# Graph attention over 16 batches: whole-array matmuls gathered into three blocks of a batch, and the layernorm split over two engines

## The chip, the core and the metric

The kernel runs on one core of a Trainium2 chip. Its engines are TensorE (matmuls and transposes, PE in the profile), VectorE (DVE), ScalarE (ACT), GpSimd (POOL) and SyncE (SP, which here only issues DMAs). The metric is device time of one execution in microseconds: 2637.62 us, the median of three runs (2637.59 to 2637.79). A difference of about 0.2% is what such runs can tell from no change.

## What is computed

Two residual layers over x of 16 batches x 1024 nodes x 256 channels, in float32, each followed by a layernorm over the channels. The change lies in the first layer and at the seam to the second:

```
fea = transpose(x)                                  # per batch: channels x nodes
c = mean(fea, axis=1)
diff = c[:, None, :] - c[:, :, None]
A = abs(abs(sigmoid(diff) - 0.5) - 0.5) * 2.0       # symmetric weights from means
g = relu(einsum('bcn,bnm->bcm', fea, adj * A_s) * para)
q = heads(transpose(g));  k, v = heads(x @ kv_w)    # 4 heads of 64
out = softmax(q k^T * scale) v
x = layernorm(x + out)
# layer 1
x = layernorm(x + batchnorm(relu(batchnorm((A_hat x) W1^T + b1)) W2^T + b2))
```

## The kernel before

**Units and bursts.** Attention of a batch is cut into 32 units: two pairs of heads (pr), two halves of the queries (qh), eight key chunks of 128 (m). `scores` (L895) makes a 128 x 1024 tile of scores with four matmuls that each use a 64 x 64 quarter of the array, and ScalarE takes the exponential (L908) into a tile p (four buffers). `outputs` (L911) multiplies p by the values, again on quarters (L924), and VectorE adds p into an accumulator acc for the denominators (L931, L933). In the profile every float32 matmul is recorded twice, and a group of quarters runs side by side. Two units make a burst, sixteen bursts (u = 0 to 15) a batch. In each burst the scores of burst j come first and then the outputs of burst j - 1 (`back`, L1135), so that the exponentials have the time of a group of outputs.

**Whole-array work.** Between bursts stands work that uses the whole 128 x 128 array, for the batch after the current one (its `steps`) and the one after that (its `first`):

- `transpose_x` (L758): four groups of four transposes, x to xT. Before the first, `begin` (L743) sums x over the channels on VectorE and sends the means through DRAM, to come back as a row on all partitions (crow).
- `values` (L848) and `keys` (L836): four groups each, v and kT, copied out of PSUM by VectorE and ScalarE.
- `graph_mm` (L797): the product of x with the weights wg, in four parts for each of the four (c, half) results; each result is 128 x 512 in one PSUM bank, and `queries` (L812) takes it out: VectorE multiplies by para (L814), ScalarE takes the relu (L817).
- `normalise` (L940): ones times acc, the sums over keys (den), which go through DRAM to lie as columns (dcol). `residual` (L964): four transposes of the output oT (poT), a multiplication by the reciprocal on VectorE (o, L974, one buffer), and an addition into x on GpSimd (L979).

The weights wg are the `side` work, on ScalarE (`weights_abs` L782, `weights_tanh` L787) and VectorE (`weights_adj` L791), eight tiles each.

`finish_x1` (L981) is the layernorm of a batch: eight statistics and aggregations on VectorE, two operations on GpSimd for the reciprocal root (L587, L589), eight subtract-and-multiply on VectorE (L600); then a DMA to DRAM, and only after this can the x of a later batch be loaded into the buffer.

**PSUM.** Three pools of two buffers each: s (two banks a buffer, scores and some others), t (one bank: transposes, v, k, graph results, den, poT) and o (one bank, the outputs).

**What sets the order.** The order of TensorE, ScalarE and VectorE is the order of the calls (`manual_schedule`); each engine's program is in that order, and an instruction waits on semaphores for what it needs. The loop over bursts gives the bursts u = 0, 4, 6, 8, 10 and 12 (`FULL`) each a block of four steps, with transposes of the next x at u = 10 and 12, the residuals four bursts after their last unit (at u = 4 and 12), and the layernorm at u = 5, between two bursts. The side work is in u = 13, 14, 15, 0, 1, 2, 3 and 4.

**The last two batches.** Batch 14 has no later x to transpose; it takes on sums of adj's rows and of its diagonal (`adjacency_rows` L1038, `adjacency_diagonal` L1031, both on VectorE). Batch 15 has no graph work; in its bursts 0, 4, 6 and 8 stand transposes of adj (`transpose_adjacency` L1041, tiles pah, copied out by ScalarE). After the last burst come the first product of layer 1 (`aggregate_first` L1092), the last residuals and the layernorm of batch 15, and then layer 1, whose bound is again TensorE.

Of the kernel before, what the change touches and what calls it, by code (L numbers as in the profile page):

```python
# [10 lines left out]
F32 = mybir.dt.float32  # L11
I32 = mybir.dt.int32
AF = mybir.ActivationFunctionType
ALU = mybir.AluOpType
# [4 lines left out]
P = 128  # L19
# [496 lines left out]
def fast_path(  # L516
# [46 lines left out]
    def tile_t(name):  # L563
        return psum["t"].tile([P, HALF], F32, tag="t", name=name)
# [26 lines left out]
    def layernorm(t, name):  # L591
# [7 lines left out]
        for n in range(NCH):  # L599
            nc.vector.tensor_scalar(  # L600
                t[:, n, :], t[:, n, :], mv[:, n, 0:1], rstd[:, n : n + 1], ALU.subtract, ALU.mult
            )

    def products(name, bank, out, mm, temps, bias):

        t = {}

        def add(dst, ps, src, b):
            if b is None:
                nc.vector.tensor_add(dst, ps, src)
            else:
                nc.vector.scalar_tensor_tensor(dst, ps, b, src, op0=ALU.add, op1=ALU.add)

        up, low = bias or (None, None)

        def p1():
            t["a"] = bank(f"a_{name}")  # L620
            mm(1, t["a"], True)
            t["p1"] = temps("p1", name)
            nc.scalar.copy(t["p1"], t["a"])

        def p6():
            t["b"] = bank(f"b_{name}")
            mm(6, t["b"], True)
            t["u2"] = temps("u2", name)
            add(t["u2"], t["b"], t["p1"], up)

        def p2():
            mm(2, t["a"], False)
            if up is None:
                nc.scalar.copy(out[0], t["a"])
            else:
                nc.scalar.activation(out[0], t["a"], AF.Identity, bias=up)

        def p7():
            mm(7, t["b"], False)
# [60 lines left out]
    with (  # L700
# [2 lines left out]
        tc.tile_pool(name="pp", bufs=4) as pp,  # L703
        tc.tile_pool(name="accp", bufs=2) as accp,
        tc.tile_pool(name="rdp", bufs=1) as rdp,
        tc.tile_pool(name="op", bufs=3) as op,
    ):
        adj_s = adjp.tile([P, NCH, N], F32, tag="adj", name="adj_s")
        para_s = pap.tile([P, CC, N], F32, tag="pa", name="para_s")
# [23 lines left out]
        def prologue(b):  # L733
# [6 lines left out]
            def step(f, *a):  # L740
                steps.append((f, a))
# [14 lines left out]
                nc.sync.dma_start(s["crow"], c_d[b][0].partition_broadcast(P))  # L756

            def transpose_x(c, half):  # L758
                if c == 0 and half == 0 and b:
                    begin()  # L760
                if c == 0 and half == 0:
                    s["xT"] = xTp.tile([P, CC, N], F32, tag="xT", name=f"xT_{b}")
                pt = tile_t(f"pxT_{b}_{c}_{half}")
                for j in range(4):
                    nc.tensor.transpose(
                        pt[:, j * P : (j + 1) * P], xt[:, 4 * half + j, c * P : (c + 1) * P], ident
                    )
                nc.vector.tensor_copy(s["xT"][:, c, half * HALF : (half + 1) * HALF], pt)

            def row_of_means():  # L770

# [22 lines left out]
                    w, w, 1.0, adj_s[:, n, :], op0=ALU.subtract, op1=ALU.mult  # L794
                )

            def graph_mm(c, half, part):  # L797
                if part == 0:
                    s["pg"] = tile_t(f"pg_{b}_{c}_{half}")
                    if c == 0 and half == 0:  # L800
                        s["qT"] = qkv.tile([P, CC, N], F32, tag="qT", name=f"qT_{b}")
                ps = s["pg"]
                hs = slice(half * HALF, (half + 1) * HALF)
                for n in (2 * part, 2 * part + 1):
# [43 lines left out]
            def values(pair):  # L848
                if pair == 0:
                    s["v"] = qkv.tile([P, NCH, C], F32, tag="v", name=f"v_{b}")  # L850
                pt = tile_t(f"pv_{b}_{pair}")
                for j in range(2):
                    n = 2 * pair + j
                    for c in range(CC):
                        nc.tensor.matmul(  # L855
                            pt[:, j * C : (j + 1) * C], s["xT"][:, c, n * P : (n + 1) * P],
                            kvw_s[:, c, C : 2 * C], start=(c == 0), stop=(c == CC - 1),
                        )
                nc.vector.tensor_copy(
                    s["v"][:, 2 * pair : 2 * pair + 2, :].rearrange("p n c -> p (n c)"), pt  # L860
                )

            for i in range(2 * CC):
                first.append((transpose_x, (i // 2, i % 2) if b else (i % 2, i // 2)))
            if b == 0:
                first += [(begin, ()), (row_of_means, ())]
            for i in range(4):
                step(values, i)
                step(keys, i // 2, i % 2)
            for c in range(CC):  # L870
                for half in range(2):
                    for part in range(4):
                        if b:
                            step(graph_mm, c, half, part)
# [89 lines left out]
        def residual(b, pr, qh):  # L964
# [13 lines left out]
            xs = s["x"][:, 4 * qh : 4 * qh + 4, pr * P : (pr + 1) * P]  # L978
            nc.gpsimd.tensor_tensor(xs, xs, o.rearrange("p n h d -> p n (h d)"), ALU.add)  # L979

        def finish_x1(b):  # L981
            xt = st.pop(b)["x"]
            layernorm(xt, f"l0_{b}")
            nc.gpsimd.dma_start(x1_d[b], xt)

        def run(fs, k):
            for f, a in fs[:k]:
                f(*a)
            del fs[:k]
# [118 lines left out]

        BURST = 2
        bursts = [range(i, i + BURST) for i in range(0, len(units), BURST)]
        PERB = PER // BURST
        FULL = (0, 4, 6, 8, 10, 12)
        SIDE = {13: 2, 14: 2, 15: 2, 1: 2, 2: 2, 3: 2}
        with tc.manual_schedule(engines={mybir.EngineType.PE, mybir.EngineType.Activation, mybir.EngineType.DVE}):


# [3 lines left out]
            for _ in range(8):  # L1122
                run(steps, 1)
                run(side, 2)
            run(next_first, 4)
            for n in range(NCH):
                run(side, 2)
                run(steps, 1)
# [1 line left out]
                    run(next_side, 3)  # L1130
            run(next_side, 99)
            run(next_steps, 8)
            full, sums, late = {}, {}, {}

            def back(j):  # L1135

                for i in bursts[j]:
                    outputs(i)
                b, pr, qh, m = units[bursts[j][-1]]
                if m == NCH - 1 and qh == 1:  # L1140
                    sums.setdefault(j + 1, []).append((normalise, (b, pr)))
                    for q in range(2):
                        full.setdefault(j + 5, []).append((residual, (b, pr, q)))
                    if pr == PAIRS - 1:
                        late.setdefault(j + 6, []).append((finish_x1, (b,)))

            last = {
                0: [(transpose_adjacency, (m, h)) for m in (0, 1) for h in (0, 1)],
# [8 lines left out]
                15: [(scale_adjacency, (0,))],  # L1157
            }
            before_last = {
                6: [(adjacency_rows, (n,)) for n in (0, 1, 2)] + [(load_weights, ())],  # L1160
                8: [(adjacency_rows, (n,)) for n in (3, 4, 5)],
                10: [(adjacency_rows, (n,)) for n in (6, 7)],
                12: [(adjacency_diagonal, ())],
            }
            for j in range(len(bursts)):
                b, u = j // PERB, j % PERB
# [7 lines left out]
                run(late.get(j, []), 9)  # L1174
# [21 lines left out]
                run(sums.get(j, []), 9)  # L1196
            j = len(bursts)
            back(j - 1)
            for m in range(NCH):
                if m + 1 < NCH:  # L1200
                    scale_adjacency(m + 1)
                aggregate_first(m)
                run(sums.get(j + m - 1, []), 9)
                run(full.get(j + m, []), 9)
            for i in range(NCH // 2):
                adjacency_sums(i)
            run(late.get(j + 5, []), 9)

    attention_psum.close()

# [421 lines left out]
```

## Time and profile before

| what | value |
|---|---|
| time, median of three | 2637.62 us |
| profiled span | 2635.9 us |
| TensorE matmul busy | 2572.7 us, 98% |
| VectorE busy | 1587.8 us, 60% |
| ScalarE busy | 1110.2 us, 42% |
| GpSimd busy | 338.9 us, 13% |
| first score of batch 3 to first score of batch 4 | 104.91 us |
| of this: busy TensorE, VectorE, ScalarE | 104.32, 66.51, 54.74 us |

The profile page gives the busy share of each engine, a chain of what ended last, and groups of equal instructions with their mean duration and the idle time ahead of them. The timeline lists the instructions of a stretch in order of time: start, length of the merged piece, engine, line, output <- inputs, shape, count, and in brackets the idle time ahead of it and who ended it. "issue" in a bracket means that the profile shows no wait. A busy TensorE isn't a TensorE without gaps, since the end of a matmul is overlapped with the start of the next: distances from start to start tell more than busy time.

### The profile page before, as it was taken

Reading aid. Unit: us, or ns where it says so; the run is one execution under the profiler, and the core shown is the slowest. Engines: PE = TensorE matmul, PEld = TensorE weight load, DVE = VectorE, ACT = ScalarE, POOL = GpSimd, SP = SyncE. Lnnn points to the kernel's source line nnn. Section 1 sums busy time; section 2 is a strip of 40 time slices with the busy share of each in tenths; the row PEclk is TensorE's granted clock in tenths of the full one; section 3 lists DMA queues with packets and bytes.
Section 4 is the critical chain, followed back from the end, with each engine's and each line's share of the span. In section 5 each row is a group of like instructions: output and inputs, shape, how many; then the busy total and the mean of one; then the engine's idle time right before and its main releaser. Section 6 shows DMA issues by size and latency. Waiting matters only on the chain. (4 is left out here: it accounts for less than half of the span.)

```text
span 2635.9 us, 32325 instructions
## 1 busy us (share of the span) xinstructions
PE 2572.7 (98%) x13158; PEld 1118.6 (42%) x13158; DVE 1587.8 (60%) x2159; ACT 1110.2 (42%) x1321; POOL 338.9 (13%) x407
## 2 busy tenths in 40 slices
PE   8999999999999999999999999999999999999986
PEld 4443444444434444444344443334444444444455
DVE  5465665756656657566566576766565565533367
ACT  5363563644635636546356364501100111133358
POOL 0001000100000001001000010232221122000036
PEclk9999999999999999999999999999999999999999
DMA  4001101011011010110110110112222222254458
GB/s 144 2 9 41 33 10 41 17 25 33 9 41 33 10 41 19 23 33 9 41 33 9 41 49 2 41 55 89 96 76 84 86 90 96 96 201 150 159 194 303
DMA packets 134557, 168.96 MB, mean 64 GB/s; under 512 B 86784, under 2 KB 120064, under 8 KB 124032
## 3 DMA queue, kind: packets, MB, share of 16 engines
q1 hardware_dynamic: 129568, 116.47, 14.1%
q0 software_dynamic: 4832, 50.34, 4.6%
q8 instruction: 105, 1.72, 0.3%
q14 instruction: 52, 0.43, 0.0%
HBM read 99.36 MB, written 67.44 MB: 63 GB/s over the span
## 5 line engine op out<-in xcount | busy, mean ns | idle before, releaser
L908 ACT ACTIVATE p<-ps 128x1024 f32<-128x1024 f32 x512 | 495.6, 1020 | 179.7 <-PE ps L903 132.6
L933 DVE TENSOR_TENSOR acc<-acc,p 128x1024 f32<-128x1024 f32 x384 | 483.2, 1258 | 60.9 <-ACT p L908 32.3
L903 PE MATMUL ps<-qT,kT 64*64 64x512 f32 x4096 | 490.5, 594 | 1.4 <-ACT p L908 1.4
L924 PE MATMUL po<-p,v 64*64 64x512 f32 x4096 | 485.3, 589 | 0.0
L805 PE MATMUL pg<-wg,x 128*128 128x512 f32 x960 | 425.2, 596 | 0.0
L979 POOL TENSOR_TENSOR x<-x,o 128x512 f32<-128x512 f32 x64 | 109.5, 1711 | 1434.8 <-DVE o L974 1434.8
L924 PEld LDWEIGHTS po<-p,v 64*64 64x64 f32 x4096 | 156.7, 133 | 282.8 <-issue 282.6
L805 PEld LDWEIGHTS pg<-wg,x 128*128 128x128 f32 x960 | 177.6, 190 | 226.9 <-issue 203.3
L903 PEld LDWEIGHTS ps<-qT,kT 64*64 64x64 f32 x4096 | 146.1, 132 | 280.2 <-issue 231.5
L817 ACT ACTIVATE qT<-qT 128x512 f32<-128x512 f32 x64 | 40.1, 630 | 481.9 <-DVE qT L814 481.9
L1457 PE MATMUL po<-hl,w12T 128*128 128x512 f32 x512 | 222.0, 596 | 3.6 <-ACT hl L1387 2.8
L814 DVE SCALAR_TENSOR_TENSOR qT<-pg,para_s 128x512 f32<-128x512 f32 x64 | 43.9, 689 | 270.7 <-PE pg L805 269.8
L793 DVE SCALAR_TENSOR_TENSOR wg<-wg,adj_s 128x1024 f32<-128x1024 f32 x128 | 153.1, 1217 | 16.0 <-ACT wg L789 16.0
L1457 PEld LDWEIGHTS po<-hl,w12T 128*128 128x128 f32 x512 | 97.7, 191 | 127.9 <-issue 120.4
L784 ACT ACTIVATE wg<-crow,ccol 128x1024 f32<-128x1024 f32 x128 | 146.6, 1146 | 12.2 <-DMA crow<-c 12.2
L789 ACT ACTIVATE wg<-wg 128x1024 f32<-128x1024 f32 x128 | 135.5, 1059 | 2.6
L1387 ACT ACTIVATE hl<-hl,bn_sh,bn_sg 128x1024 f32<-128x1024 f32 x64 | 74.4, 1229 | 137.4 <-DMA hl<-h 136.1
L855 PE MATMUL pv<-kvw_s,xT 128*128 128x256 f32 x512 | 124.0, 385 | 1.6 <-ACT kT L846 1.6
L1468 DVE TENSOR_SCALAR o<-po,col_b 128x1024 f32<-128x1024 f32 x31 | 39.8, 1283 | 138.1 <-PE po L1457 138.1
L842 PE MATMUL pk<-xT,kvw_s 128*128 128x512 f32 x256 | 120.3, 592 | 0.0
L855 PEld LDWEIGHTS pv<-kvw_s,xT 128*128 128x128 f32 x512 | 94.9, 190 | 51.9 <-issue 27.6
L1286 PE MATMUL b_agg<-aT,x1S 128*128 128x512 f32 x240 | 109.2, 598 | 0.0
(159 smaller groups left out, 2641.4 us busy)
## 6 DMA issues: line engine op xcount, KB each, us to landing
h<-hw POOLq DMA_DIRECT2D x16, 2048.0 KB, 6.6
hl<-h SPq DMA_DIRECT2D x15, 2048.0 KB
x<-x POOLq DMA_DIRECT2D x16, 1024.0 KB, 4.2
x1l<-x SPq DMA_DIRECT2D x16, 1024.0 KB
xf<-x SPq DMA_DIRECT2D x16, 1024.0 KB
out_dram<-o SPq DMA_DIRECT2D x16, 1024.0 KB
x<-in_x_dram SPq DMA_DIRECT2D x15, 1024.0 KB
crow<-c SPq DMA_DIRECT2D x15, 512.0 KB
```

The lines of the kernel that those rows point to most:

```text
L784: nc.scalar.activation(w, s["crow"], AF.Abs, bias=s["ccol"][:, n : n + 1])
L789: nc.scalar.activation(w, w, AF.Tanh, scale=0.5)
L793: nc.vector.scalar_tensor_tensor(w, w, 1.0, adj_s[:, n, :], op0=ALU.subtract, op1=ALU.mult)
L805: nc.tensor.matmul(ps, xt[:, n, c * P : (c + 1) * P], s["wg", n][:, hs], start=(n == 0), stop=(n == NCH - 1),)
L842: nc.tensor.matmul(ps, kvw_s[:, c, kc * P : (kc + 1) * P], s["xT"][:, c, hs], start=(c == 0), stop=(c == CC - 1),)
L855: nc.tensor.matmul(pt[:, j * C : (j + 1) * C], s["xT"][:, c, n * P : (n + 1) * P], kvw_s[:, c, C : 2 * C], start=(c == 0), stop=(c == CC - 1),
L903: nc.tensor.matmul(ps[kh * D : (kh + 1) * D, hd * HALF : (hd + 1) * HALF], kT[r, pr, ks], qT[r, pr, qh * HALF : (qh + 1) * HALF], start=Tr ...
L908: nc.scalar.activation(p, ps, AF.Exp)
L924: nc.tensor.matmul(g["po"][kh][hd * D : (hd + 1) * D, :], s["v"][r, m, h * D : (h + 1) * D], p[r, hd * HALF : (hd + 1) * HALF], start=(m = ...
L933: nc.vector.tensor_add(g["acc"], g["acc"], p)
L979: nc.gpsimd.tensor_tensor(xs, xs, o.rearrange("p n h d -> p n (h d)"), ALU.add)
L1457: nc.tensor.matmul(ps[:, hs], w2T[:, k, c * P : (c + 1) * P], h[k][:, hs], start=(k == 0), stop=(k == HC - 1),)
```

## The change

The whole-array work of a batch is gathered into three blocks, after the bursts u = 0, 4 and 8. It is for fewer changes between quarters and whole array. Its parts:

- **u = 0**: seven of the eight v and k groups, with the denominators of the batch before and its four residuals (both pairs of heads) between them, and the rest of the side work.
- **u = 4**: the graph product of c = 0, all of it, then the eighth group (the last k). The layernorm of the batch before stands around it: statistics ahead of the block, and the scaling after four of its steps.
- **u = 8**: two transposes of the next x, half the graph product of c = 1, two more transposes, the other half, then den of the first pair.
- **Side work** moves to u = 9 to 15 (two items each) and u = 0.
- **Graph results** are 128 x 1024 in a buffer of pool s in place of 128 x 512 in pool t; VectorE and ScalarE take each out in one operation of 1024 columns in place of two of 512.
- **Layernorm** is split (`layernorm_steps`): statistics on VectorE, four operations on GpSimd in place of two (also minus mean times scale), and the scaling by eight ACTIVATE on ScalarE in place of eight VectorE operations.
- **Copies**: half of the xT copies and half of the v copies go from VectorE to ScalarE, from batch 1 on.
- **oT** has four buffers in place of three, since the first pair's residuals wait for u = 0 of the next batch.
- **Batch 14 and 15**: row sums go to u = 8, 10, 11, 12, 13 and the diagonal to u = 15; the lists of batch 15 stay, with its first pair's residuals at u = 12. `full`, `sums` and `late` are lists in order of entry in place of tables by burst.

```diff
+    def layernorm_steps(t, name):
...
+        def statistics():
+            for n in range(NCH):
+                nc.vector.bn_stats(st[:, n, :], t[:, n, :])
+                nc.vector.bn_aggr(mv[:, n, :], st[:, n, :])
+            rsqrt(rstd, mv[:, :, 1], EPS)
+            nc.gpsimd.tensor_tensor(nmr, mv[:, :, 0], rstd, ALU.mult)
+            nc.gpsimd.tensor_scalar(nmr, nmr, -1.0, None, ALU.mult)
+
+        def apply():
+            for n in range(NCH):
+                nc.scalar.activation(
+                    t[:, n, :], t[:, n, :], AF.Identity,
+                    bias=nmr[:, n : n + 1], scale=rstd[:, n : n + 1],
+                )
...
-        tc.tile_pool(name="op", bufs=3) as op,
+        tc.tile_pool(name="op", bufs=4) as op,
...
-                nc.vector.tensor_copy(s["xT"][:, c, half * HALF : (half + 1) * HALF], pt)
+                copy = nc.scalar.copy if half and b else nc.vector.tensor_copy
+                copy(s["xT"][:, c, half * HALF : (half + 1) * HALF], pt)
...
-            def graph_mm(c, half, part):
-                if part == 0:
-                    s["pg"] = tile_t(f"pg_{b}_{c}_{half}")
...
+            def graph_mm(c, n):
+                if n == 0:
+                    s["pg"] = tile_s(f"pg_{b}_{c}")
...
+                for hs in (H0, H1):
                     nc.tensor.matmul(
-                        ps, xt[:, n, c * P : (c + 1) * P], s["wg", n][:, hs],
+                        s["pg"][:, hs], xt[:, n, c * P : (c + 1) * P], s["wg", n][:, hs],
                         start=(n == 0), stop=(n == NCH - 1),
                     )
-                if part == 3:
-                    queries(c, hs, ps)
+                if n == NCH - 1:
+                    queries(c, slice(0, N), s["pg"])
...
+                copy = nc.scalar.copy if pair % 2 and b else nc.vector.tensor_copy
...
-        FULL = (0, 4, 6, 8, 10, 12)
-        SIDE = {13: 2, 14: 2, 15: 2, 1: 2, 2: 2, 3: 2}
...
             before_last = {
-                6: [(adjacency_rows, (n,)) for n in (0, 1, 2)] + [(load_weights, ())],
-                8: [(adjacency_rows, (n,)) for n in (3, 4, 5)],
-                10: [(adjacency_rows, (n,)) for n in (6, 7)],
-                12: [(adjacency_diagonal, ())],
+                6: [(load_weights, ())],
+                8: [(adjacency_rows, (n,)) for n in (0, 1, 2, 3)],
+                10: [(adjacency_rows, (4,))],
+                11: [(adjacency_rows, (5,))],
+                12: [(adjacency_rows, (6,))],
+                13: [(adjacency_rows, (7,))],
+                15: [(adjacency_diagonal, ())],
             }
...
-                if u in FULL:
-                    if u >= 10:
-                        run(next_first, 1)
-                    for _ in range(4 if b or u > 4 else 0):
-                        run(steps, 1)
-                        if u <= 4:
-                            run(side, 2)
-                    if u >= 10:
-                        run(next_first, 1)
-                    run(full.get(j, []), 9)
-                elif u > 12:
-                    run(next_side, SIDE[u])
-                else:
-                    run(side, SIDE.get(u, 0))
+                if u == 0:
+                    for i in range(7):
+                        if b:
+                            run(steps, 1)
+                            run(side, 1 if i < 4 else 2)
+                        if i == 1:
+                            run(sums, 1)
+                        if i in (2, 3, 5):
+                            run(full, 1)
+                    run(side, 99)
+                    run(full, 1)
+                elif u == 4:
+                    run(late, 1)
+                    keys_last = steps[:1] if b else []
+                    del steps[: len(keys_last)]
+                    for n in range(NCH):
+                        run(steps, 1)
+                        if n == 3:
+                            run(late, 1)
+                    run(keys_last, 1)
+                elif u == 8:
+                    run(next_first, 3)
+                    for n in range(NCH):
+                        run(steps, 1)
+                        if n == 3:
+                            run(next_first, 2)
+                    run(sums, 1)
+                elif u > 8:
+                    run(next_side, 2)
...
+                    if u == 12:
+                        run(full, 2)
```

More of the change, by code (lines that the diff above doesn't have):

```diff
@@ L602, in layernorm @@
             )
+    def layernorm_steps(t, name):
+        st = small.tile([P, NCH, 6], F32, tag="ln_st", name=f"st_{name}")
+        mv = small.tile([P, NCH, 2], F32, tag="ln_mv", name=f"mv_{name}")
+        rstd = small.tile([P, NCH], F32, tag="ln_rs", name=f"rs_{name}")
+        nmr = small.tile([P, NCH], F32, tag="ccol", name=f"nm_{name}")
+        def statistics():
[11 more added lines that the diff above has]
+                )
+        return statistics, apply
     def products(name, bank, out, mm, temps, bias):
@@ L758, in transpose_x @@
             def transpose_x(c, half):
-                if c == 0 and half == 0 and b:
-                    begin()
                 if c == 0 and half == 0:
@@ L795, in weights_adj @@
                 )
-            def graph_mm(c, half, part):
-                if part == 0:
-                    s["pg"] = tile_t(f"pg_{b}_{c}_{half}")
-                    if c == 0 and half == 0:
+            def graph_mm(c, n):
+                if n == 0:
+                    s["pg"] = tile_s(f"pg_{b}_{c}")
+                    if c == 0:
                         s["qT"] = qkv.tile([P, CC, N], F32, tag="qT", name=f"qT_{b}")
-                ps = s["pg"]
-                hs = slice(half * HALF, (half + 1) * HALF)
-                for n in (2 * part, 2 * part + 1):
+                for hs in (H0, H1):
                     nc.tensor.matmul(
-                        ps, xt[:, n, c * P : (c + 1) * P], s["wg", n][:, hs],
+                        s["pg"][:, hs], xt[:, n, c * P : (c + 1) * P], s["wg", n][:, hs],
                         start=(n == 0), stop=(n == NCH - 1),
                     )
-                if part == 3:
-                    queries(c, hs, ps)
+                if n == NCH - 1:
+                    queries(c, slice(0, N), s["pg"])
             def queries(c, hs, ps):
@@ L858, in values @@
                         )
-                nc.vector.tensor_copy(
-                    s["v"][:, 2 * pair : 2 * pair + 2, :].rearrange("p n c -> p (n c)"), pt
-                )
+                copy = nc.scalar.copy if pair % 2 and b else nc.vector.tensor_copy
+                copy(s["v"][:, 2 * pair : 2 * pair + 2, :].rearrange("p n c -> p (n c)"), pt)
             for i in range(2 * CC):
@@ L866, in prologue @@
                 first += [(begin, ()), (row_of_means, ())]
+            else:
+                first.insert(0, (begin, ()))
             for i in range(4):
@@ L869, in prologue @@
                 step(keys, i // 2, i % 2)
[L870 to L874, printed above, removed]
+            for c in range(CC if b else 0):
+                for n in range(NCH):
+                    step(graph_mm, c, n)
             for n in range(NCH if b == 0 else 0):
@@ L979, in residual, with statistics_x1 @@
             nc.gpsimd.tensor_tensor(xs, xs, o.rearrange("p n h d -> p n (h d)"), ALU.add)
+        def statistics_x1(b):
+            statistics, st[b]["ln"] = layernorm_steps(st[b]["x"], f"l0_{b}")
+            statistics()
         def finish_x1(b):
-            xt = st.pop(b)["x"]
-            layernorm(xt, f"l0_{b}")
-            nc.gpsimd.dma_start(x1_d[b], xt)
+            s = st.pop(b)
+            s["ln"]()
+            nc.gpsimd.dma_start(x1_d[b], s["x"])
         def run(fs, k):
@@ L1124, in fast_path @@
                 run(side, 2)
-            run(next_first, 4)
+            run(next_first, 5)
             for n in range(NCH):
@@ L1132, in fast_path @@
             run(next_steps, 8)
-            full, sums, late = {}, {}, {}
+            full, sums, late = [], [], []
             def back(j):
@@ L1140, in back @@
                 if m == NCH - 1 and qh == 1:
-                    sums.setdefault(j + 1, []).append((normalise, (b, pr)))
+                    sums.append((normalise, (b, pr)))
                     for q in range(2):
-                        full.setdefault(j + 5, []).append((residual, (b, pr, q)))
+                        full.append((residual, (b, pr, q)))
                     if pr == PAIRS - 1:
-                        late.setdefault(j + 6, []).append((finish_x1, (b,)))
+                        late.append((statistics_x1, (b,)))
+                        late.append((finish_x1, (b,)))
             last = {
@@ L1173, in fast_path @@
                     back(j - 1)
-                run(late.get(j, []), 9)
                 if u == 5 and b + 2 < B:
@@ L1177, in fast_path @@
                     next_first, next_steps, next_side = prologue(b + 2)
-                if u in FULL:
-                    if u >= 10:
-                        run(next_first, 1)
-                    for _ in range(4 if b or u > 4 else 0):
-                        run(steps, 1)
-                        if u <= 4:
-                            run(side, 2)
-                    if u >= 10:
-                        run(next_first, 1)
-                    run(full.get(j, []), 9)
-                elif u > 12:
-                    run(next_side, SIDE[u])
-                else:
-                    run(side, SIDE.get(u, 0))
+                if u == 0:
[14 more added lines that the diff above has]
+                    for n in range(NCH):
+                        run(steps, 1)
+                        if n == 3:
[3 more added lines that the diff above has]
+                    run(next_first, 3)
+                    for n in range(NCH):
+                        run(steps, 1)
[4 more added lines that the diff above has]
+                    run(next_side, 2)
                 if b == B - 2:
@@ L1195, in fast_path @@
                     run(last.get(u, []), 9)
-                run(sums.get(j, []), 9)
+                    if u == 12:
+                        run(full, 2)
             j = len(bursts)
@@ L1202, in fast_path @@
                 aggregate_first(m)
-                run(sums.get(j + m - 1, []), 9)
-                run(full.get(j + m, []), 9)
+                if m == 1:
+                    run(sums, 1)
+                if m == 4:
+                    run(full, 2)
             for i in range(NCH // 2):
                 adjacency_sums(i)
-            run(late.get(j + 5, []), 9)
+            run(late, 2)
     attention_psum.close()
```

## The prediction

> **What bounds the kernel now.** I read the busy shares first, then TensorE's timeline of one middle batch, then the waits of the other engines.
>
> ```profile
> PE 2572.7 (98%) x13158; PEld 1118.6 (42%) x13158; DVE 1587.8 (60%) x2159; ACT 1110.2 (42%) x1321; POOL 338.9 (13%) x407
> L908 ACT ACTIVATE p<-ps 128x1024 f32<-128x1024 f32 x512 | 495.6, 1020 | 179.7 <-PE ps L903 132.6
> ```
>
> TensorE is the bound throughout, so only the gaps between its matmuls can be won. Its timeline (start, length) around one whole-array block of a batch (u = 4):
>
> ```profile
> 395.95 1.90 PE L924 MATMUL po<-p,v 64*64 64x512 f32 x16
> 397.78 1.99 PE L855 MATMUL pv<-kvw_s,xT 128*128 128x256 f32 x8
> 399.61 1.88 PE L842 MATMUL pk<-xT,kvw_s 128*128 128x512 f32 x4
> 401.33 1.89 PE L855 MATMUL pv<-kvw_s,xT 128*128 128x256 f32 x8
> 403.06 1.88 PE L842 MATMUL pk<-xT,kvw_s 128*128 128x512 f32 x4
> 404.77 0.60 PE L970 MATMUL poT<-ident,oT 128*128 128x128 f32 x4
> 405.61 0.66 PE L970 MATMUL poT<-ident,oT 128*128 128x128 f32 x4 [0.24 <-ACT kT L846]
> 406.20 1.95 PE L903 MATMUL ps<-qT,kT 64*64 64x512 f32 x16
> 407.97 1.90 PE L924 MATMUL po<-p,v 64*64 64x512 f32 x16
> ```
>
> Start to start, 512 columns take 0.429 us, so a group of scores or outputs takes 1.72, a v or k group 1.72, a group of four 128-column transposes 0.436. What exceeds this is loss. po to pv: 397.78 - 395.95 - 1.72 = 0.11, and pv runs 0.10 long: 0.21 to enter. poT to ps: 0.59 - 0.44 = 0.15 to leave. The second poT starts 0.84 after the first, not 0.44: 0.40 spent waiting for a bank that ACT must empty. Summed over batch 3 in this way: entries and exits 6 x 0.3 to 0.36, two den groups with 0.14 more each, 0.46 and 0.57 at the two places where poT follows a k group or a pxT group: **3.55 us of the 104.9 us** that each batch from 1 to 13 takes.
>
> ScalarE where weights are made (u = 13 to 15 now):
>
> ```profile
> 677.84 1.94 ACT L908 ACTIVATE p<-ps 128x1024 f32<-128x1024 f32 x2 [1.79 <-PE ps L903]
> 679.67 1.15 ACT L784 ACTIVATE wg<-crow,ccol 128x1024 f32<-128x1024 f32 x1
> 680.85 1.06 ACT L789 ACTIVATE wg<-wg 128x1024 f32<-128x1024 f32 x1
> 681.81 1.92 ACT L908 ACTIVATE p<-ps 128x1024 f32<-128x1024 f32 x2
> ```
>
> Two exponentials, an abs and a tanh take 3.97 us where TensorE's burst takes 3.43: ScalarE falls 0.54 behind per such burst. At 680 it is not behind; two bursts later it is 1.1 us behind, and TensorE still does not stop.
>
> [...] the trace shows no overtaking, and my largest costs rest on this. [...] after a 2.04 us gap, six matmuls take 0.85 us each; a 1.94 us gap does nothing[...].
>
> ```profile
> 1759.95 1.57 PE L1318 MATMUL b_h<-tT,w12T 128*128 128x512 f32 x2 [1.88 <-DVE u_h L615]
> 1761.31 4.04 PE L1286 MATMUL b_agg<-aT,x1S 128*128 128x512 f32 x6
> ```
>
> **Part by part, a middle batch.** Whole-array matmul work stays the same. I walked the changed program's queues, engine by engine, with durations of the rows above; zero is the end of the last po slot before a block.
>
> *Three entries and exits go* (3 x 0.36), as do the two poT waits at the old places (0.46, 0.57).
>
> *Block u = 0* now holds pv, pk, den, pv, poT, pk, poT, pv, pk, poT, pv, poT. PSUM pool t has two banks, taken in turn, so a group waits for the drain of the group before last. Where only a poT (0.44) lies between, a bank needs 0.84 (0.20 to the copy, 0.58 copy, 0.06 back) and TensorE waits 0.40, as at 405.61. That happens three times: pk after v1, pv after kT01, pv after kT10; each with 0.06 of restart. Block: entry 0.21, den between full groups 0.34, waits 1.38, exit 0.15: **2.08**. The denominators' return is hidden: dcol lands 3.4 to 6.2 us after drow in the trace, and is asked for 8 us after it.
>
> *Block u = 4*: 16 pg pairs, the kept key group, exit: **0.36**. The key group (1.72) hides the drain of pg's two banks (0.20 + about 1.23: between 1.22, the SBUF row L793, and 1.28, the PSUM row L1468). The layernorm lies under 13.7 us of pg: statistics 8 x 0.53 after oT, to 5.7; GpSimd chain (0.24 and 1.67 in the rows below, two more at about 0.3) to 8.6; eight ACTIVATE to 12.4. Nothing visible.
>
> ```profile
> 413.69 0.24 POOL L587 TENSOR_SCALAR rs_l<-mv_l 128x8 f32<-128x8 f32 x1 [3.20 <-DVE mv_l L597]
> 414.02 1.67 POOL L589 TENSOR_TENSOR rs_l<-rs_l,mhalf 128x8 f32<-128x8 f32 x1
> ```
>
> Price of an ACTIVATE 128x256 with scale and bias columns: 0.56 alone and about 0.47 in a row (L1570, same form). [...] Moving it frees DVE of 2.7 us and of 2.1 us waiting for GpSimd, which cost TensorE nothing before.
>
> *Block u = 8*: pxT, pg, pxT, pg, den: **0.45**. But its end loads ScalarE: relu of 1024 columns (about 0.97 in a row) and drow (0.48) stand ahead of the exponentials, which start 0.6 late. Then come abs and tanh in u = 9, 10 (3.97 each), abs in u = 11. Lag: 0.6, 1.2, 1.75; TensorE's slack is about 1.2 us, so it stops once, at u = 12: 0.50 + 0.05. **0.55**, bounds 0 and 1.2. The row crow lands 18.0 to 20.4 us after the block began (sum and DMA issue 4.05; c to crow issue 8.7 to 11.2, crow 3.3 to 5.6 in the trace, sums 14.0 to 16.4) and is wanted at 20.4: just hidden.
>
> Sum: 2.08 + 0.36 + 0.45 + 0.55 = 3.44 against 3.55: **-0.1 per batch, -1.4 for thirteen**.
>
> **The ends.** Batch 0 has fewer exits, but no key group after pg (0.5): -0.9. Batch 14 loses its 1.26 wait before u = 15 scores: -1.5. Start-up: the same waits, 0.
>
> Batch 15, u = 0: four poT and four pah now stand without v and k groups between. The diagonal sums (eight pairs, 2.7 to 3.6 us on DVE) now stand in u = 15 ahead of the last acc additions, so den waits about 2 us. Then poT by poT through DVE and GpSimd (2.07 from one o to the next, 2.75 when GpSimd's addition takes 2.19) and dcol, which is asked for at once. Loss about 10 against 1.4: **+8.5**.
>
> Batch 15, u = 4: there are no graph matmuls left to shade the layernorm. Its eight ACTIVATE stand in ScalarE's queue ahead of the copies that free pah's banks. pah 0 and 1 run at 0.1 to 1.0; pah 2 waits for ScalarE: to 12.4, then the copy, 13.05. With half-rate after it (up to 1.7) the loss is about 14 against the 3.4 of the poT and pah waits now there: **+10.5**.
>
> Batch 15's own layernorm, at the start of layer 1: DVE no longer stops for GpSimd and eight tensor_scalar (1754.3 to 1759.2), so the 2.04 gap and its half rate go: **-3.5**; ScalarE's copies behind it are not wanted soon.
>
> Total: -1.4 - 0.9 - 1.5 + 8.5 + 10.5 - 3.5 = +11.7, so **2649**.
>
> **Rivals.** *Within noise, 2642*: ScalarE's lag never reaches TensorE, so a batch gains 0.66 (-8.6 in place of -1.4). For it: now the same lag of 1.1 us costs nothing. Against: relu and drow come first.
> *Faster, 2624*: the bank waits of u = 0 do not occur either, so a batch gains 3.55 - 1.5 = 2.05: -26.7, with the ends +13.1. For it: entries and exits are real. Against: 405.61 shows the very wait, and the new order has three such places.
> *Slower still, 2662*: crow misses its 20.4 or the lag feeds through p and DVE, 1 us more per batch: +13. For it: crow's margin is 0 to 2.4 us.
>
> **How the numbers follow.** Forecast 0.55, within noise 0.16, faster 0.10, slower still 0.19. Range 2639 to 2660: it takes in ScalarE's lag from 0 to 1.2 (-7 to +8) and the ends within 3. Over 0.2% slower is above 2642.9: forecast and last rival, 0.74; same 0.16; faster 0.10.
>
> **What would show it.** Middle batch 104.8 us; in u = 0, pk or pv groups starting 0.4 late with ACT v or ACT kT as releaser, three per batch; scores at u = 12 waiting for ACT p by 0.5; stretches at u = 0 and u = 4 of the last batch with TensorE idle for 2 to 12 us, pah waiting for ACT ahT behind the layernorm. Wrong if middle batches take 103 us or less (bank waits), or if pah in u = 4 is not held.

## The result, and the profile after

The changed kernel takes 2651.9 us (median; 2651.1 to 2653.4) against 2637.7 us before: ratio 1.0055, 95% interval 1.0037 to 1.0072. It is 14.2 us slower; 2649 was forecast. Executions of the kernel before fall into two groups (of 53 in all sets of runs, 12 took 2633.1 to 2633.9 us and 41 took 2636.6 to 2638.5), and the four compared here are all of the second, so against the first the changed kernel is some 18 us slower. From the page of the changed kernel (busy shares; then for a group: busy time, mean ns of one, and the idle time ahead of it with who ended it):

```profile
PE 2571.6 (97%) x13158; PEld 1124.0 (42%) x13158; DVE 1513.3 (57%) x1941; ACT 1204.1 (45%) x1479; POOL 346.8 (13%) x439
L877 PE MATMUL pv<-kvw_s,xT 128*128 128x256 f32 x512 | 126.9, 391 | 8.3 <-ACT kT L868 8.3
L864 PE MATMUL pk<-xT,kvw_s 128*128 128x512 f32 x256 | 121.8, 598 | 3.3 <-ACT v L882 3.3
L622 ACT ACTIVATE x<-x,nm_l,rs_l 128x256 f32<-128x256 f32 x128 | 64.6, 586 | 120.0 <-POOL nm_l L618 120.0
```

VectorE gave up 75 us and ScalarE took 94; TensorE's busy time is as before, so the 14 us are gaps. Three lines show where: v and k groups now wait for ScalarE's copies of kT and v, and ScalarE itself stands still for 120 us in all for GpSimd, ahead of the scalings. Where the time lies, from the starts of TensorE's instructions in the two profiled executions (which differ by 15.7 us):

| stretch | before | after | difference |
|---|---|---|---|
| start to the first score | 75.46 | 76.32 | +0.9 |
| batch 0, first score to first score | 86.99 | 85.80 | -1.2 |
| batches 1 to 13 | 13 x 104.90 | 13 x 104.95 | +0.6 |
| batches 14 and 15, to the last score | 178.07 | 198.99 | **+20.9** |
| last score to the third a_agg group of layer 1 | 78.93 | 75.09 | -3.8 |
| from there to the last po of layer 2 | 750.14 | 748.37 | -1.8 |
| last po to the last matmul | 86.42 | 86.51 | +0.1 |

So the loss is in the last batch (+22.3 us, 0.86 of it work that moved there; batch 14 is 1.4 shorter), and the change in the middle is worth nothing, which is not the same as doing nothing. TensorE in u = 0 of a middle batch:

```profile
382.03 0.60 PE L991 MATMUL poT<-ident,oT 128*128 128x128 f32 x4
382.87 1.98 PE L864 MATMUL pk<-xT,kvw_s 128*128 128x512 f32 x4 [0.24 <-ACT v L882]
384.69 0.60 PE L991 MATMUL poT<-ident,oT 128*128 128x128 f32 x4
385.53 1.99 PE L877 MATMUL pv<-kvw_s,xT 128*128 128x256 f32 x8 [0.24 <-ACT kT L868]
387.36 1.88 PE L864 MATMUL pk<-xT,kvw_s 128*128 128x512 f32 x4
389.07 0.60 PE L991 MATMUL poT<-ident,oT 128*128 128x128 f32 x4
389.91 1.99 PE L877 MATMUL pv<-kvw_s,xT 128*128 128x256 f32 x8 [0.24 <-ACT kT L868]
```

From poT to the next group it is 0.84 us where four transposes need 0.43, three times; the group after such a stop runs another 0.10 long (1.98 and 1.99 against 1.88). The one poT that is followed by no stop, the fourth, ends the block. Losses, start to start, of this batch: u = 0 2.23, u = 4 0.36, u = 8 0.45, u = 12 0.54: 3.58 (3.55 before). At u = 12 the scores wait for ScalarE:

```profile
463.12 2.01 PE L924 MATMUL ps<-qT,kT 64*64 64x512 f32 x16 [0.23 <-ACT p L929]
```

In u = 0 of the last batch TensorE waits three times for the multiplication o (1.42, 1.59 and 1.41 us), and after the last of these waits it runs at half rate (twelve transposes, 0.21 us from one to the next in place of 0.11, and three of the four matmul steps of the scores behind them, 0.85 to 0.90 us in place of 0.43), which costs about 2.9 us:

```profile
1643.89 3.01 PE L1071 MATMUL pah<-ident,adj_s 128*128 128x128 f32 x12 [1.41 <-DVE o L995]
1646.83 3.27 PE L924 MATMUL ps<-qT,kT 64*64 64x512 f32 x16
```

In u = 4 of the last batch, TensorE and ScalarE:

```profile
1662.04 1.09 PE L1071 MATMUL pah<-ident,adj_s 128*128 128x128 f32 x8
...
1671.34 4.04 ACT L622 ACTIVATE x<-x,nm_l,rs_l 128x256 f32<-128x256 f32 x8 [8.58 <-POOL nm_l L618]
...
1676.00 1.97 PE L1071 MATMUL pah<-ident,adj_s 128*128 128x128 f32 x8 [12.87 <-ACT ahT L1074]
```

ScalarE waits 8.58 us for GpSimd, then scales for 4.04, and only then copies the pah tiles that TensorE waits for: 12.87 us of idle TensorE, after which two pah groups take 1.97 instead of 1.09.

Loss of a stretch of the last batch below is its length, start to start of the last po ahead of the two blocks, less the work in it (3.43 a burst, 0.43 a poT or pah group, 0.86 den). u = 0: 28.32 - 18.02 = 10.3 (before 17.76 - 16.30 = 1.5). u = 4: 24.03 - 8.58 = 15.4 (before 12.90 - 9.43 = 3.5).

### The profile page after: what moved, and what is told of

Its sections match the earlier page's. It is cut to its first block, busy times and chain, and to the rows that moved or that the text cites. A ratio compares the mean times of both kernels' runs of the same rounds, so it can differ in the third digit from the quotient of the medians.

```text
span 2651.6 us, 32316 instructions
## 1 busy us (share of the span) xinstructions
PE 2571.6 (97%) x13158; PEld 1124.0 (42%) x13158; DVE 1513.3 (57%) x1941; ACT 1204.1 (45%) x1479; POOL 346.8 (13%) x439
## 3 DMA queue, kind: packets, MB, share of 16 engines
q8 instruction: 105, 1.72, 0.3%
## 4 chain that ended last, share of the span: by engine, by line
PE 77%; DVE 9%; ACT 8%; issue 3%; DMA 2%; POOL 1%; ACTq 0%; SPq 0%; DVEq 0%; POOLq 0%
PE pg L827 15%; PE ps L924 14%; PE po L945 13%; PE po L1503 8%; PE pv L877 5%; PE pk L864 4%; PE b_agg L1332 4%; PE c_agg L1332 4%; PE b_h L1364 2%; ACT p L929 2%; PE a_agg L1332 2%; PE c_h L1364 2%; ACT wg L808 1%; DMA c<-ncol 1%; ACT o L1545 1%
## 5 line engine op out<-in xcount | busy, mean ns | idle before, releaser
L817 DVE SCALAR_TENSOR_TENSOR wg<-wg,adj_s 128x1024 f32<-128x1024 f32 x128 | 163.2, 1278 | 22.9 <-ACT wg L813 22.9
L836 DVE SCALAR_TENSOR_TENSOR qT<-pg,para_s 128x1024 f32<-128x1024 f32 (+1 forms) x34 | 39.2, 1160 | 236.2 <-PE pg L827 235.0
L622 ACT ACTIVATE x<-x,nm_l,rs_l 128x256 f32<-128x256 f32 x128 | 64.6, 586 | 120.0 <-POOL nm_l L618 120.0
L959 DVE TENSOR_TENSOR oT<-po,oT 128x512 f32<-128x512 f32 x64 | 44.2, 691 | 124.4 <-ACT oT L958 124.4
```

The lines of the kernel that those rows point to most:

```text
L817: nc.vector.scalar_tensor_tensor(w, w, 1.0, adj_s[:, n, :], op0=ALU.subtract, op1=ALU.mult)
```

## The experiments

Ratios are to the kernel before, in the same set of runs. Beside the whole time I give the **attention stretch**, from the first score to the last: 1628.8 us before, 1649.1 after. It leaves out the start (first score at 74.1 to 76.3 us in the profiles) and what follows the last score, which vary for other reasons (last section). All are edits of the changed kernel but one, which says so.

**The scalings of the last batch behind pah.** In batch 15 `run(late, 1)` moves from the fourth step of u = 4 to behind the pah groups:

```diff
-                        if n == 3:
+                        if n == 3 and b < B - 1:
                             run(late, 1)
...
+                    if u == 4:
+                        run(late, 1)
```

> In the last batch alone the eight scalings of the layernorm are called after the four pah groups of u = 4. Theory (ScalarE's strict queue is the cause, and the eight ACTIVATE stand ahead of whatever follows): pah is free at once, but the exponentials of u = 5 now stand behind the scalings, which end 12.4 us after the block began; TensorE has 1.5 + 3.5 us of work left before it needs them, so the stop moves to the scores of u = 6 and shrinks from 13 to about 7.5 us: -4 to -5 us in all, 2647. Rival (only the order of the pah copies was wrong): the loss of that stretch falls back to the 3.4 us of before, -12 us, 2640. Rival (the stop at pah hides another one behind it): no change, 2652.

Ratio 1.0053 (1.0038 to 1.0068); attention stretch -5.0, the loss of u = 4 15.4 to 10.9. TensorE:

```profile
1664.75 1.90 PE L945 MATMUL po<-p,v 64*64 64x512 f32 x16
1674.68 3.57 PE L924 MATMUL ps<-qT,kT 64*64 64x512 f32 x16 [8.04 <-ACT p L929]
```

The stop moved to the scores of u = 6, which now wait for exponentials that stand behind the scalings. ScalarE:

```profile
1669.68 4.04 ACT L622 ACTIVATE x<-x,nm_l,rs_l 128x256 f32<-128x256 f32 x8 [5.91 <-POOL nm_l L618]
```

The scores of u = 5 started at 1662.98 us, their exponentials only at 1673.63, right behind the scalings. So it is ScalarE's queue, not pah's place in it. The whole time alone would not have shown this: its interval holds both no gain and the 4.5 expected.

**The layernorm of batch 14 on VectorE.** `statistics_x1` calls the old `layernorm` if b == 14.

> The layernorm of batch 14 alone (the one that falls into u = 4 of the last batch) is done on VectorE as in the kernel before; all others stay split. Theory: ScalarE has nothing of it in its queue, the stretch of u = 4 of the last batch loses about 3.4 us instead of 15.4: -12 us, 2640; the scores of u = 5 and 6 don't wait for VectorE. Rival (VectorE's queue then stops the accumulations and, through p, the exponentials): -5 us or less, 2647 or more.

2643.6 us, 1.0029 (1.0017 to 1.0041): -8.3 us, attention stretch -10.0. Between the two expectations. u = 4 loses 1.0, less than the 3.4 of the theory, but u = 6 got a stop of its own (timeline of all engines):

```profile
1669.23 2.67 DVE L600 TENSOR_SCALAR x<-x,mv_l,rs_l 128x256 f32<-128x256 f32 x8 [2.12 <-POOL rs_l L589]
...
1673.15 1.94 ACT L929 ACTIVATE p<-ps 128x1024 f32<-128x1024 f32 x2 [6.04 <-DVE acc L952]
...
1675.72 1.70 PE L1075 MATMUL pah<-ident,adj_s 128*128 128x128 f32 x8 [3.58 <-ACT ahT L1078]
```

With no graph product to hide under, VectorE's additions wait behind the layernorm, the four p buffers fill, the exponentials stop, and the pah copies behind them.

**The scalings in two fours, at u = 7 and 9.** Last batch only; the store of x and the load of layer 1's second x follow them to u = 9:

```diff
+                    if u in (7, 9):
+                        st[b - 1]["ln"](range(4 * (u // 9), 4 * (u // 9) + 4))
...
```

> Last batch alone: the layernorm of batch 14 stays split as in the changed kernel, but of its eight ACTIVATE four are called at u = 7 and four at u = 9 instead of all in u = 4; the load of the second x of layer 1 moves from u = 7 to u = 9, behind the store. Theory (what hurts is a ScalarE queue that stands still for GpSimd, not the work itself; a burst leaves ScalarE 1.4 us, four ACTIVATE are 2.0): the stretch of u = 4 loses 1.0 us instead of 15.4, u = 6 is free too, u = 7 and 9 put ScalarE 0.6 behind, which is inside its slack: -14 us, 2638. Rival (VectorE or GpSimd, not ScalarE's queue, set that stop, as VectorE did when it had the whole layernorm): -8 us or less, 2644.

2641.1 us, 1.0015 (1.0009 to 1.0022): -10.8. Attention stretch -14.6, as expected; u = 4 loses 1.0 and u = 6 1.0. ScalarE:

```profile
1676.81 2.07 ACT L622 ACTIVATE x<-x,nm_l,rs_l 128x256 f32<-128x256 f32 x4
1678.78 1.92 ACT L929 ACTIVATE p<-ps 128x1024 f32<-128x1024 f32 x2
```

No wait ahead of the scalings, none of TensorE behind them. The same eight ACTIVATE cost 14 us or next to nothing, by where they stand. (Of the 4 us between stretch and total, 1.6 and 1.4 are the two places of the last section.)

**poT in the outputs' pool.**

```diff
-            pt = tile_t(f"poT_{k}")
+            pt = tile_o(f"poT_{k}")
```

> The transposes poT take their bank from the pool of the outputs, which is free where they stand, instead of the two-bank pool of the v and k groups. Theory (two banks with a drain of 0.84 us and a group of 0.44 us between): the three waits of 0.40 + 0.105 in each u = 0 go: -1.5 us in each of batches 1 to 14, -21 us, 2631; period of a middle batch 103.4 us. Rival (the copies of v and kT are late because ScalarE is busy with weights and exponentials, so the wait returns at the next v or k group): period 104.5 or more, at most -6 us. Rival (poT now waits for the outputs' drain): one wait of about 1 us in each batch instead of three, -7 us, 2645.

2645.5 us, 1.0039 (1.0026 to 1.0053); period 104.74. The three waits are gone, and one has come that is nearly as dear:

```profile
390.36 1.02 PE L945 MATMUL po<-p,v 64*64 64x512 f32 x2
391.63 1.51 PE L945 MATMUL po<-p,v 64*64 64x512 f32 x11 [0.25 <-DVE o L995]
```

The first outputs of u = 1 take the bank of the last poT, which the multiplication o has not yet left. Worse than the 0.41 us of waiting: one quarter of the array has started alone, and its first matmul (the two records, 0.86 us) runs beside nothing. 1.53 saved, 1.32 lost, 0.21 a batch left. My third expectation had the number (2645) and the one wait in place of three, but the wait the other way round: the outputs wait for a bank of poT, not poT for a bank of the outputs.

**The same, the last two residuals one group earlier**, so that a v group (1.72 us) stands between the last poT and the outputs:

```diff
-                        if i in (2, 3, 5):
+                        if i in (2, 3, 4, 5):
                             run(full, 1)
                     run(side, 99)
-                    run(full, 1)
```

> As the kernel with poT in the pool of the outputs, but each residual stands one group earlier where it was last: after the second v, the second k, the third v and the third k group, so that the last v group (1.72 us) stands between the last poT and the outputs that take its bank. That kernel had lost its three bank waits (1.53 us) but had got a wait of 0.41 us at the second quarter of the first outputs, in which one quarter runs alone (0.86 us more). Theory: this goes as well, period 104.95 - 1.5 = 103.4, -21 us in batches 1 to 14 and -4 us in the last: 2627. Rival (the bank of po is held by the multiplication o, which waits for the columns that are now asked for 2 us earlier): period 104.4 or more, 2640 or more.

2629.8 us, 0.9973 (0.9961 to 0.9984); period 103.43 in every batch, 1.52 less. TensorE:

```profile
384.00 0.60 PE L991 MATMUL poT<-ident,oT 128*128 128x128 f32 x4
384.43 1.89 PE L877 MATMUL pv<-kvw_s,xT 128*128 128x256 f32 x8
386.25 1.95 PE L924 MATMUL ps<-qT,kT 64*64 64x512 f32 x16
388.02 1.90 PE L945 MATMUL po<-p,v 64*64 64x512 f32 x16
```

The bank waits were what u = 0 lost beyond its entry, den and exit: of its 2.23 us 0.7 are left, and two small edits took the rest away. This is faster than the kernel before.

**One piece of weight work at u = 9**, and in a second run at u = 9 and u = 12:

```diff
-                    run(next_side, 2)
+                    run(next_side, 1 if u in (9, 12) else 2)
```

That is the second run; the first has `u == 9` in this place.

> At u = 9 one piece of weight work is called instead of two; the rest follow one place later, the last in u = 0. Theory (relu and drow at the end of u = 8 and two bursts of abs and tanh put ScalarE 1.75 us behind): it is then about 1 us less behind, the stop of 0.41 at u = 12 with its after-effects, 0.54 in all, goes: -0.5 us in each of batches 0 to 13, -7 us, 2645; period 104.4 us. Rival (the stop comes from something else at u = 12, or ScalarE's slack is smaller than 1.2 us): no change, 2652.

> One piece of weight work at u = 9 and at u = 12, two at the other bursts; the rest in u = 0. With one piece fewer at u = 9 alone the stop had gone from u = 12 to u = 14, behind the oT copy of u = 12, which keeps ScalarE waiting for the outputs with an abs and a tanh behind it. Theory (ScalarE's debt, two exponentials with abs and tanh needing 3.97 us of a burst of 3.43): no stop from u = 9 to 15, period 104.4, -7 us, 2645. Rival (the debt only moves again, to u = 14 or 15 or into u = 0): period 104.9, no change.

The first: 2652.8 us, 1.0062 (1.0048 to 1.0076), period 105.00: my theory's -0.5 did not come. The stop had moved from u = 12 to u = 14:

```profile
466.31 0.59 ACT L958 COPY oT<-po 128x512 f32<-128x512 f32 x1 [0.62 <-PE po L945]
466.79 1.15 ACT L808 ACTIVATE wg<-crow,ccol 128x1024 f32<-128x1024 f32 x1
467.97 1.06 ACT L813 ACTIVATE wg<-wg 128x1024 f32<-128x1024 f32 x1
```

At u = 12 ScalarE stands still for the outputs, copies oT, and with an abs and a tanh behind that it is late again. The second run takes one piece away there too: 2645.9 us, 1.0031 (1.002 to 1.0043), period 104.48, -0.47 a batch, no stop left from u = 9 to 15. So the prediction's cause (relu and drow, then abs and tanh) was half of it; a rested ScalarE would have made up a debt once, and a second debt follows.

**u = 0 cut in two.** Its last two v and k groups and residuals go to u = 2 in batches 0 to 14: a fourth block.

```diff
-                    for i in range(7):
+                    for i in range(7 if b == B - 1 else 5):
...
+                elif u == 2 and b < B - 1:
+                    for i in (5, 6):
...
```

> The block of u = 0 is cut in two in batches 0 to 14: its last two v and k groups with the last two residuals go to u = 2, so that a batch has four blocks instead of three; the same work otherwise. Theory (an entry and an exit cost 0.36 us by the trace): period of a middle batch 104.95 + 0.36 = 105.3, in all +5 us, 2657. Rival (the first block then ends on a poT of which nothing waits, one bank wait of 0.51 goes and pays for the new block): period 104.8, no change in all. Rival (what the blocks cost is hidden, and fewer blocks are worth nothing): period 104.95.

2658.5 us, 1.008 (1.0066 to 1.0093), period 105.31: +0.36, to the hundredth the price of an entry and an exit as read off the trace. The three bank waits stayed.

**The last batch's u = 0.** Two residuals and two pah groups go to u = 2, in turn, and the diagonal to u = 3:

```diff
+                3: [(adjacency_diagonal, ())],
...
-                15: [(adjacency_diagonal, ())],
...
+                if b == B - 1 and u in (0, 2):
+                    if u == 0:
+                        run(sums, 1)
+                    for _ in range(2):
+                        run(full, 1)
+                        run(first_pah, 1)
+                elif u == 0:
...
```

> Last batch alone: two of the four residuals and two of the four pah groups of u = 0 go to u = 2, residual and pah in turn, and the sums of the diagonal go from u = 15 of batch 14 to u = 3 of the last. Theory (den waits for the diagonal, poT for the one o buffer and for columns asked for at once): the stretch of u = 0 falls from 9.4 us of loss to about 2, and u = 2 adds about 1.2: -6 us in all, 2646; in the trace the time from the first to the last score of the last batch is 6 us less. Rival (the wait for o and GpSimd returns at u = 2 as it was): -2 us or less.

2647.2 us, 1.0039 (1.0026 to 1.0053); attention stretch -7.2. u = 0 loses 1.4 and u = 2 1.0 instead of 10.3 together, but u = 4 0.9 more: the sums of the diagonal, now at u = 3, hold up VectorE's oT, so that the statistics begin 2.9 us after the block and not 1.4. How much each of the moves gave is not separated.

**The layernorm of batches 0 to 13 on VectorE**, whole, at u = 4.

> The whole layernorm on VectorE at the place of the statistics (u = 4) for batches 0 to 13, whose layernorm falls under the graph product; batches 14 and 15 stay split as in the changed kernel. Theory (under 13.7 us of graph product neither VectorE's nor ScalarE's part is waited for, so in these batches the split is worth nothing): period 104.95, no change in all, 2652. Rival (VectorE's queue, 4.2 us of statistics, 2.1 of waiting for GpSimd and 2.7 of scaling, stops the accumulations and with them p and the scores of u = 5): period 105.5 or more, 2660 or more.

2650.7 us, 1.0057 (1.0041 to 1.0072), period 104.95 as before the edit. Under 13.7 us of graph product it makes no difference here which engine scales.

**The kernel before, with the same care for poT.** poT in the outputs' pool, and the residuals after the second group of their block:

```diff
+            pt = tile_o(f"poT_{k}")
...
-                    for _ in range(4 if b or u > 4 else 0):
+                    for k in range(4 if b or u > 4 else 0):
+                        if k == 2 and b < B - 1:
+                            run(full.get(j, []), 9)
                         run(steps, 1)
```

> The kernel before with the same care for poT: its bank comes from the outputs' pool, and the two residuals of a block stand after its second group instead of after its last (in the last batch they stay last). Theory: the waits of 0.40 to 0.51 at both places of each batch go, 1.0 us a batch, period 103.9, -14 us, 2624. Then three blocks instead of six are worth, at equal bank waits, 103.9 - 103.4 = 0.5 us a batch with ScalarE's stop of 0.54 and 1.0 without it. Rival (in the kernel before the waits are not those of the bank): period 104.9, no change.

2615.2 us, 0.9924 (0.9911 to 0.9938): -22, more than the 14 expected. Period 103.72, 1.18 less than before.

```profile
397.19 1.04 PE L970 MATMUL poT<-ident,oT 128*128 128x128 f32 x8
398.06 1.89 PE L855 MATMUL pv<-kvw_s,xT 128*128 128x256 f32 x8
```

No wait at the two poT (the pair, 0.87 us start to start, took 1.43 with its stop and exit before). Thirteen batches give 15.4; the attention stretch is 18.1 shorter, since batches 0 and 14 have such waits as well (0.7 and 2.4). Behind the last score a wait of 1.3 us for VectorE's ahT is gone, while u = 12 and 13 of the last batch lose as much. The remainder can't be credited to the edit: half rate at the start of layer 1 (1.7 us) and of layer 2 (1.7), in the profile of the kernel before and not in this one, of which more below.

**Everything together**: poT early in the outputs' pool (batch 14's second pair excepted), weight work, the last batch's u = 0 and scalings.

> Together: poT in the outputs' pool, one group earlier (-21 in batches 1 to 14); one piece of weight work at u = 9 and 12 (-0.47 in each of 14 batches, -6.5); the residuals and pah of the last batch's u = 0 shared with u = 2 and the diagonal later (-5 to -6); the ACTIVATE of batch 14 at u = 7 and 9 (-14). If these are separate waits they add up: 2652 - 46 = 2605, period 103.0. Rival (they share waits, so that one stop comes back where another is taken away): 2615 or more.

2609.3 us, 0.9898 (0.9883 to 0.9914), period 103.32, attention stretch 1604.7, 44.4 less than the changed kernel's; the whole time is 42.6 less where 46 were expected. The causes nearly add up, save that TensorE stops once more, for 0.31 us and 0.11 of restart, at the scores of u = 2: the weight work taken from u = 9 and 12 is now at the end of u = 0, where an abs and a tanh stand behind the last v copy and ahead of the exponentials of u = 1. It is faster than both kernels.

## Why the prediction was right, point by point

- **Middle batch**, 3.44 expected, 3.58 measured, period 104.95 where 104.8 was said. Three bank waits of 0.40, where they were said to be and with the releasers said; the restart after each took 0.105, not 0.06: that is the missing 0.13. Moving poT's bank and place removed these 1.53 us (1.52), so the cause is shown. u = 4 and u = 8 as forecast (0.36, 0.45). With this the thirteen batches cost 0.6 us where a gain of 1.4 was forecast.
- **ScalarE's stop at u = 12**, 0.55 expected, 0.54 measured. Shown by removing it, but only in the second attempt: the oT copy at u = 12 adds a second debt that I had not counted.
- **Layernorm in the shade**: nothing visible in batches 0 to 13, and the run with VectorE in its place shows that the split is worth nothing there either.
- **Batch 15, u = 0**: +8.5 expected, +8.8 measured (10.3 against 1.5). poT behind o came as said. But den lost only 0.45 us by its wait where about 2 were said, and the half rate (2.9) was not in this term, so that the total came so close is in part luck. **u = 4**: +10.5 expected, +12.0 measured. The mechanism is shown by three runs. The size was short: GpSimd's chain from the last statistics to its result took 3.6 us, not 2.9 (its first operation 1.12 instead of the 0.24 of a middle batch; why is open), eight ACTIVATE 4.04, not 3.8, and the half rate after the stop reached the scores of u = 5 (2.92 us from their start to that of the outputs, in place of 1.72).
- **Layer 1**: -3.5 expected, -3.8 measured; argued from the trace alone. The 2.04 gap is gone, and with it 1.7 us of half rate (four matmul records at about 0.85 in place of 0.43, not the six of the prediction). The second part can't be put down to the split for certain: the kernel before with poT in the outputs' pool scales on VectorE too and has the same gap, but no half rate behind it. So the size of the gap does not decide, as the prediction had taken it to do:

```profile
1739.24 1.12 PE L1320 MATMUL b_h<-tT,w12T 128*128 128x512 f32 x2 [1.88 <-DVE u_h L615]
```

- **Batch 0 and 14**: the residuals of the first pair now fall into the next batch, so 0.86 us of work (two poT groups) leave batch 0 in the table and enter batch 15. Without it batch 0 gained 0.3 where 0.9 were forecast. The 1.26 wait of batch 14 is gone as forecast: -1.4, where -1.5 was said.
- **Not in the sum**: +0.9 at the start, though other kernels with the changed kernel's start had their first score between 74.1 and 76.1, so no cause in the change is shown; and -1.8 in layer 2, for which none is shown either (last section). Most terms above came out dearer than forecast, so that the total lies this near is in part owed to these 1.8 us.
- **Rivals.** "Faster" needed the bank waits not to occur; with them out of the way the kernel does become faster, 2629.8. "Within noise" needed ScalarE's lag to be free: it costs 0.47 a batch. crow was not late: ScalarE's only wait of more than 0.3 us for it was at the start, before the first score.

What gathering six blocks into three is worth, with all that goes with it and at equal care for poT: 103.72 against 103.32, **0.4 us a batch**. A block more costs 0.36, but the three blocks saved only 0.8 in all (entries, exits and den add up to 2.35 in the old order without bank waits and to 1.51 in the new), since den stands in the middle of whole-array work (0.34) and the transposes' entries had cost only 0.32; the other 0.4 goes to ScalarE's lateness after u = 0 (the stop at u = 2 and its restart).

## What to carry to other kernels

A short group in a two-bank pool cost the next group the rest of the drain (0.40 us behind four transposes of 0.43), so when work is gathered into fewer blocks, look at which groups become neighbours of a short one; give it another pool, and a long group behind it before that pool's owner returns (1.52 us a batch here). An operation moved to an engine with spare time was free here only where nothing that others need stood behind it while it waited for a third engine: under 13.7 us of graph product the scalings cost nothing (period 104.95 on either engine), in u = 4 of the last batch, where ScalarE waits 8.58 us for GpSimd, the loss grew by 12.0. So check the last iteration, where the work that shaded it is missing. Before crediting a restructuring, give the old kernel the same repairs: here the old order with a bank exchanged and the residuals moved is within 6 us of the best.

## What the runs showed that was not expected

- At the start of layer 2 TensorE is idle for about 3 us, and behind that the matmuls of the kernel before run at half rate for a while and those of the changed kernel do not. The gaps (start to start, less the 0.43 of the matmul before) are 3.01 and 2.95 us. The first line is of the kernel before, where three records in a row start 0.85 us after the one ahead of them, the second of the changed one, where they start 0.43 apart:

```profile
2325.99 6.25 PE L1457 MATMUL po<-hl,w12T 128*128 128x512 f32 x10 [2.85 <-ACT hl L1387]
```

```profile
2343.23 6.28 PE L1503 MATMUL po<-hl,w12T 128*128 128x512 f32 x14 [2.79 <-ACT hl L1433]
```

  Ten matmul records against fourteen in the same time: 1.7 us, the most of the -1.8 us of layer 2 in the table. The length of the gap alone does not tell which it will be: in layer 1 (above) half rate came after a gap of 2.04 us, in one kernel of the two that have it, and here it did not come after 2.95. What decides is not shown.
- From the last po to the last matmul it is 86.4 to 86.5 us in the profiles of six kernels and 87.6 to 88.0 in those of the other eight, with the same code there. What chooses between the two is not settled. With the point above (1.7 us there, 1.1 to 1.6 here), two kernels that differ elsewhere can differ by 3 us for no reason that their edits show, so gains of a few us are better read from the stretch that was edited.
- A wait inside a group of matmuls that share the array by quarters cost more than its length: 0.41 us of wait made 1.32 of loss (poT in the outputs' pool).
